# Carrying a run's last quarter of output and the next run's transposed tokens over the loop's back edge

## The chip, the core and the metric

The kernel runs on one NeuronCore of a Trainium2 chip. The metric is the device time of one execution in microseconds (us). Before the change it was 9271.71 us, the median of three runs (9268.06 to 9273.82).

The engines are called by these names: TensorE (PE in the profile, with its weight loads as PEld), VectorE (DVE), ScalarE (ACT), GpSimd (POOL) and SyncE (SP). SP issues the plain transfers. GpSimd issues the indirect ones: gathers of rows by a list of row numbers, and scatters to such rows.

## What is computed

The input is 4 x 1024 tokens of 1024 channels in float32. First an attention-like layer changes every token; then a mixture of experts with 8 experts does, each token going to its best two. The kernel's time lies almost wholly in the second part. Cut to what matters:

```python
x = x + xattn(layernorm(x), ctx_512, W_k, b_k, ln_gamma, ln_beta)   # first part, about 500 us
h = layernorm(x)                                                    # 4096 tokens of 1024
probs = softmax(h @ gate_w)                                         # 8 experts
topk_w, topk_idx = top_k(probs, 2);  topk_w /= topk_w.sum(-1)
# for every expert e, over the tokens that chose it:
y_e = (silu(h @ w1[e]) * (h @ w3[e])) @ w2[e]                       # 1024 -> 3584 -> 1024
x = x + sum of topk_w * y_e over the token's two experts
```

## The kernel before

**First part.** Attention, normalisation and routing run tile by tile. They leave the attended tokens in the output tensor (`of` in the code), the normalised tokens in `h_d`, and in `id_d` one list per expert: the token's row number, and its weight as raw bits beside it.

**Runs and blocks.** The rest of the kernel is a loop on the chip, `tc.For_i`. One pass is a run: one expert and some of its tokens. A `Switch` picks one of 13 unrolled bodies by the number of blocks in the run and their width; each body is what `run(...)` emits. With this input there are 8 runs, one for each expert, of three blocks each, with widths of 328, 336, 352 and 360 tokens. Within a body the compiler's planner orders the work of VectorE, ScalarE, GpSimd and SP by its own estimate of times; TensorE's order is the order of the code (`manual_schedule`).

At the loop's end there is a barrier: every engine arrives, semaphores are set back, and each engine branches to the loop's head, loads the next run's expert, slot and kind from small tables into registers and branches into the body. The barrier and these branches appear in the records at L784, L787 and L815.

**The products.** Every product is done in blocks of two by two with seven products instead of eight (the Winograd form of Strassen's scheme). That takes sums of the four quarters of a weight tile, by `weight_sums` (lines 573 to 577, four VectorE instructions), and sums of the four quarters of the tokens, by `token_sums` (lines 592 to 594, three instructions). The seven products go to four PSUM banks, and `combine` (lines 608 to 614) puts the four quarters of the result together with one ScalarE copy and four VectorE instructions. Half a block's width, `n`, is what one matmul streams.

**A block.** A block has two phases:

- Up: for each of 14 pairs of hidden tiles, a 1 MB tile of `w1` and one of `w3` are loaded, summed and multiplied with the tokens `x` (L735, 56 matmul records for each tile); `combine` gives `c1` and `c3`, then SiLU and product give `g`.
- Down: for each of the four output quarters `q`, four tiles of `w2` are multiplied with `g` (L766), and `combine` gives `y`.

**Tokens in.** `tokens_in` transposes the gathered `rows` on TensorE (L679), 24 transposes in six PSUM tiles, of which the pool holds two at a time. Three are copied to `x` by ScalarE (L687) and three by VectorE (L685). Then come the token sums. For the second and third block it stands after quarter 1 of the block before. For a run's first block it stands at the head of the body.

**Tokens out.** `tokens_out` transposes a quarter's `y` back (L697, six transposes in three PSUM tiles of the same pool) and adds it, times the token's weight, to the accumulator `acc` (L701). After the last quarter three scatters write `acc` to the output rows (L707). The list `late` puts this work behind the next piece of products: quarter `q` is transposed after the first weight tile of quarter `q + 1`, and the last quarter of a block after the first `w1` tile of the next block. After a run's last block it is done at once, at the end of the body. `acc` is filled by gathers from the output tensor (L638) before the down phase.

**Across the edge.** `load_first(i + 1)`, called between the phases of a run's last block, loads the next run's ids, gathers its first rows, and loads its first tiles `w1a` and `w3a`. Their sums and the transposes of the rows are made in the next pass, at the head of the body.

Of the kernel before, what the change touches and what calls it, by code (L numbers as in the profile page):

```python
# [18 lines left out]
P = 128  # L19
# [14 lines left out]
def kernel(  # L34
# [488 lines left out]

    with ExitStack() as st:
        fst = st.enter_context(tc.tile_pool(name="fst", bufs=1))
        wp = st.enter_context(tc.tile_pool(name="wp", bufs=3))
        ap = st.enter_context(tc.tile_pool(name="ap", bufs=1))
        hp = st.enter_context(tc.tile_pool(name="hp", bufs=1))  # L530
        gp = st.enter_context(tc.tile_pool(name="gp", bufs=2))
        ip = st.enter_context(tc.tile_pool(name="ip", bufs=2))
# [7 lines left out]
        RT = 3  # L540
        HK = KD // 2
        NI = KM // 2


        T1, B11, B12, B21, B22, T2, T4 = range(7)
# [12 lines left out]
            weights(t, wf, ex, k0, kn, c0)  # L558
            return t

        def weight_sums(t, kn, halves):

            n = kn // 2
            if halves:
                v = t[:, :kn, :].rearrange("p (i h) c -> p i h c", h=2)
                lo, hi = v[:, :, 0, :], v[:, :, 1, :]
            else:
                lo, hi = t[:, :n, :], t[:, n:kn, :]
            a11, a21 = lo[:, :, :P], lo[:, :, P:]
            a12, a22 = hi[:, :, :P], hi[:, :, P:]  # L570
            s = wp.tile([P, 3, HK, P], F32, tag="s", name="ws")
            s1, s2, s4 = s[:, 0, :n, :], s[:, 1, :n, :], s[:, 2, :n, :]
            nc.vector.tensor_tensor(s1, a21, a22, ALU.add)  # L573
            nc.vector.tensor_tensor(s2, s1, a11, ALU.subtract)  # L574
            nc.vector.tensor_tensor(s4, a12, s2, ALU.subtract)  # L575
            s3 = a21
            nc.vector.tensor_tensor(s3, a11, a21, ALU.subtract)  # L577
            return dict(p1=a11, p2=a12, p3=s4, p4=a22, p5=s1, p6=s2, p7=s3)

        RIGHT = dict(p1=B11, p2=B21, p3=B22, p4=T4, p5=T1, p6=T2, p7=T3)  # L580
        BANK = dict(p1=(0, 0), p2=(1, 0), p6=(1, 1), p5=(2, 0), p7=(2, 1), p3=(3, 0), p4=(3, 1))
# [14 lines left out]
        def banks():  # L596
            return [ps.tile([P, N], F32, tag="ps", name=f"ps{i}") for i in range(4)]

        def combine(pp, n, tag):

            def pair(t):
                return t[:, : 2 * n].rearrange("p (a b) -> p a b", b=n)

            def twice(v):
                return v.unsqueeze(1).to_broadcast([P, 2, n])

            p1s = gp.tile([P, n], F32, tag="p1s", name="p1s")
            nc.scalar.copy(p1s, pp[0][:, :n])  # L608
            c = gp.tile([P, 4, n], F32, tag=tag, name=tag)
            nc.vector.tensor_tensor(c[:, 0:2, :], pair(pp[1]), twice(p1s), ALU.add)  # L610
            vu = gp.tile([P, 2, n], F32, tag="vu", name="vu")
            nc.vector.tensor_tensor(vu, pair(pp[2]), twice(c[:, 1, :]), ALU.add)  # L612
            nc.vector.tensor_tensor(c[:, 1:3, :], pair(pp[3]), vu, ALU.add)  # L613
            nc.vector.tensor_tensor(c[:, 3, :], pp[2][:, :n], vu[:, 1, :], ALU.add)
            return c

        def expert(i):
            return nc.values_load(
# [29 lines left out]
        rows = [fst.tile([P, D], F32, name=f"rows{s}") for s in range(RT)]  # L648
        w1a = fst.tile([P, KD, QW], F32, name="w1a")
        w3a = fst.tile([P, KD, QW], F32, name="w3a")  # L650

        def load_rows(s0):
            load_ids(ids0, s0)
# [4 lines left out]
        def load_first(i):  # L658
            ex = expert(i)
            load_rows(first_slot(i))  # L660
            weights(w1a, w1f, ex, 0, KD, 0)
            weights(w3a, w3f, ex, 0, KD, 0)

        def run(i, ex, s0, blocks, width):
            n = width // 2
            split = [min(P, width - c) for c in range(0, width, P)]

            def tokens_in():

                ids = ip.tile([P, RT, IDW], I32, tag="ids", name="ids")  # L670
                nc.vector.tensor_copy(ids, ids0)
                rd = ip.tile([P, RT], I32, tag="rd", name="rd")
                nc.vector.tensor_copy(rd, rd0)
                x = hp.tile([P, HK, 7 * n], F32, tag="x", name="x")
                for s, r in enumerate(split):
                    for h in range(2):
                        pt = pst.tile([P, N], F32, tag="pt", name="pt_h")
                        for k in range(HK):
                            nc.tensor.transpose(  # L679
                                pt[:, ts(k, r)], rows[s][:r, ts(HK * h + k, P)], ident[:r, :r]  # L680
                            )
                        src = pt[:, : HK * r].rearrange("p (a b) -> p a b", b=r)
                        dst = x[:, :, ds((B11 + 2 * h) * n + s * P, r)]
                        if h % 2:
                            nc.vector.tensor_copy(dst, src)  # L685
                        else:
                            nc.scalar.copy(dst, src)  # L687
                xv = x.rearrange("p k (q c) -> p k q c", q=7)
                token_sums(xv, n)
                return ids, rd, xv  # L690

            def tokens_out(ids, acc, q, y):
                yv = y.rearrange("p (d h) c -> p d (h c)", h=2)
                for s, r in enumerate(split):
                    pt = pst.tile([P, N], F32, tag="pt", name="pt_y")
                    for d in range(2):
                        nc.tensor.transpose(  # L697
                            pt[:r, ts(d, P)], yv[:, d, ds(s * P, r)], ident
                        )
                    part = acc[s][:r, ts(q, QW)]  # L700
                    nc.vector.scalar_tensor_tensor(  # L701
                        part, pt[:r, :QW], ids.bitcast(F32)[:r, s, 1:2], part,
                        ALU.mult, ALU.add,
                    )
                if q == DQ - 1:
                    for s, r in enumerate(split):
                        nc.gpsimd.indirect_dma_start(  # L707
                            out=of,
                            out_offset=bass.IndirectOffsetOnAxis(
                                ap=ids[:r, s, 0:1], axis=0  # L710
                            ),
                            in_=acc[s][:r, :],
                            in_offset=None,
                            bounds_check=T - 1,
                            oob_is_err=False,
                        )

            late = []
            now = tokens_in()
            for b in range(blocks):  # L720
                ids, rd, x = now
                last = b == blocks - 1
                if not last:
                    load_rows(s0 + (b + 1) * width)
# [1 line left out]
                for i2 in range(NI):  # L726
                    cs = []
                    for wf, wa, tag in ((w1f, w1a, "c1"), (w3f, w3a, "c3")):
                        t = load(wf, ex, 0, KD, i2 * QW) if b or i2 else wa
                        left = weight_sums(t, KD, False)  # L730
                        pp = banks()
                        for p in ORDER if b or i2 else EARLY:
                            bk, half = BANK[p]
                            for k in range(HK):
                                nc.tensor.matmul(  # L735
                                    pp[bk][:, ts(half, n)], left[p][:, k, :],
                                    x[:, k, RIGHT[p], :],
                                    start=(k == 0), stop=(k == HK - 1),
                                )
                        cs.append(combine(pp, n, tag))  # L740
                        while late:
                            late.pop(0)()
                    c1, c3 = cs
                    nc.scalar.activation(c1, c1, AF.Silu)  # L744
                    nc.vector.tensor_tensor(g[:, i2, B11 : B22 + 1, :], c1, c3, ALU.mult)  # L745
                    token_sums(g[:, i2, :, :], n)

                if last:
                    load_first(i + 1)
                acc = [  # L750
                    ap.tile([P, D], F32, tag=f"acc{s}", name="acc") for s in range(len(split))
                ]
                for s, r in enumerate(split):
                    gather(acc[s][:r, :], of, rd, s, r)
                for q in range(DQ):
                    pp = banks()
                    i2 = 0
                    for kn in W2K:
# [13 lines left out]
                            i2 += 1  # L772
                        while late:
                            late.pop(0)()
                    y = combine(pp, n, "y")
                    late.append(lambda a=ids, c=acc, d=q, e=y: tokens_out(a, c, d, e))
                    if q == 1 and not last:
                        now = tokens_in()
            while late:
                late.pop(0)()  # L780

        load_first(0)
        n_run = nc.values_load(run_n, min_val=1, max_val=NRUN)
        with tc.For_i(0, n_run) as i:  # L784
            ex = expert(i)
            s0 = first_slot(i)
            kind = nc.values_load(run_k[:, ds(i, 1)], min_val=0, max_val=len(RUNS) - 1)  # L787
            for k in tc.Switch(kind, len(RUNS)):
                with tc.manual_schedule(engines={ENG.PE}):
                    run(i, ex, s0, *RUNS[k])  # L790


# [26 lines left out]
```

## Time and profile before

| what | value |
|---|---|
| median of three timed runs | 9271.71 us |
| profiled execution, its own time | 9277.28 us |
| span of that execution in the profile | 9275.4 us |
| mean granted TensorE clock | 0.977 |
| TensorE matmul busy | 8865.5 us, 96% of the span |
| VectorE busy | 5115.8 us, 55% |
| ScalarE, GpSimd busy | 694.4 us, 406.0 us |
| bytes moved by transfers | 1236.36 MB, mean 133 GB/s |

The profile is one execution. A window such as 8142.56:8177.57 is a stretch in us from the span's start. A row of windows gives the stretch's length, and then for each engine its busy time with the number of instructions in brackets, the clock that TensorE was granted (1.00 is full speed), the share of time in which the transfer engines were busy, and GB/s. A row of waits names who waited, for whom, the total in us, how often, and the longest. One fp32 matmul of the code is two records of about 0.15 us each in the trace, from start to start.

The last of the seven edges between runs, in order of time (from the sequencers' and engines' records):

| us | what |
|---|---|
| 8142.56 | last matmul of the down phase starts |
| 8143.24 | VectorE starts the last instruction of `combine` |
| 8144.94, 8151.67, 8155.84 | the three scatters start, each after the one before has landed |
| 8150.05, 8150.25 | VectorE and TensorE arrive at the barrier |
| 8164.00 | GpSimd has drained, as the last |
| 8171.01 | first transpose of the next run's tokens |
| 8177.57 | first matmul of the up phase |

### The profile page before, as it was taken

The page shows a single profiled execution, that of the slowest core. Times are in us where ns is not written, and L with a number is a line of the kernel's source. Part 1 is how long each engine was busy: PE and PEld are TensorE (multiplying, and loading weights), DVE is VectorE, ACT ScalarE, POOL GpSimd, SP SyncE. Part 2 cuts the span into 40 slices and gives each one's busy share as a digit, 9 for nine tenths or more (in the row PEclk, how much of TensorE's full clock was granted, in tenths as well). Part 3 has the DMA queues.
Part 4 walks back from the last instruction along what each step waited for, and adds up shares of the span by engine and source line. Part 5 has one row for each costly group of instructions (what it writes and reads, how often), then busy time and mean ns, then how long its engine had stood idle before and what let it go on. Part 6 is the DMA issues. An engine that isn't in the chain of part 4 may idle for free. (4 is left out here: it accounts for less than half of the span.)

```text
span 9275.4 us, 139976 instructions
## 1 busy us (share of the span) xinstructions
PE 8865.5 (96%) x59428; PEld 8665.9 (93%) x59429; DVE 5115.8 (55%) x10003; ACT 694.4 (7%) x1524; POOL 406.0 (4%) x494
## 2 busy tenths in 40 slices
PE   8979998999989999899989999899998999989999
PEld 5569998999989999899989999899998999989999
DVE  5655654655645555556546556465564565555654
ACT  3300000000000000000000000000000000000000
POOL 2310000000000000000000000000000000000000
PEclk9979999999999999999999999999999999999999
DMA  3234444344433444344434434444443344434343
GB/s 132 109 123 145 138 144 141 125 147 130 157 118 118 143 131 138 119 136 138 141 128 135 139 121 138 132 132 146 137 147 120 125 140 135 141 117 141 124 134 127
DMA packets 1116668, 1236.36 MB, mean 133 GB/s; under 512 B 34848, under 2 KB 1077280, under 8 KB 1115872
## 3 DMA queue, kind: packets, MB, share of 16 engines
q1 hardware_dynamic: 1079424, 1114.54, 37.1%
q0 software_dynamic: 31952, 107.24, 3.3%
q8 instruction: 500, 8.19, 0.4%
q10 hardware_dynamic: 4496, 3.97, 0.1%
q14 instruction: 296, 2.42, 0.1%
HBM read 1155.26 MB, written 70.65 MB: 132 GB/s over the span
## 5 line engine op out<-in xcount | busy, mean ns | idle before, releaser
L735 PE MATMUL ps<-x,wt 128*128 128x168 f32 (+3 forms) x20992 | 3285.3, 309 | 0.0
L735 PEld LDWEIGHTS ps<-x,wt 128*128 128x128 f32 x20992 | 3123.4, 190 | 0.0
L735 PE MATMUL ps<-x,ws 128*128 128x168 f32 (+3 forms) x16128 | 2571.8, 309 | 0.0
L735 PEld LDWEIGHTS ps<-x,ws 128*128 128x128 f32 x16128 | 2411.8, 190 | 0.0
L766 PE MATMUL ps<-g,wt 128*128 128x168 f32 (+3 forms) x10752 | 2031.6, 310 | 0.0
L573 DVE TENSOR_TENSOR ws<-wt 128x512 f32<-128x512 f32 (+1 forms) x1040 | 693.8, 667 | 2206.3 <-DMA wt<-in_L_ffn_w_dram 2123.3
L766 PEld LDWEIGHTS ps<-g,wt 128*128 128x128 f32 x10752 | 1693.4, 191 | 0.0
L766 PE MATMUL ps<-g,ws 128*128 128x168 f32 (+3 forms) x8064 | 1619.6, 310 | 0.0
L766 PEld LDWEIGHTS ps<-g,ws 128*128 128x128 f32 x8064 | 1299.0, 191 | 0.2 <-DVE y L610 0.2
L610 DVE TENSOR_TENSOR c<-ps,p1s 128x352 f32<-128x352 f32 (+3 forms) x672 | 346.7, 516 | 1045.1 <-PE ps L735 1016.1
L574 DVE TENSOR_TENSOR ws<-ws,wt 128x512 f32<-128x512 f32 (+1 forms) x1040 | 692.4, 666 | 30.2
L577 DVE TENSOR_TENSOR wt<-wt 128x512 f32<-128x512 f32 (+1 forms) x1040 | 685.3, 659 | 0.0
L575 DVE TENSOR_TENSOR ws<-wt,ws 128x512 f32<-128x512 f32 (+1 forms) x1040 | 684.3, 658 | 0.0
L608 ACT COPY p1s<-ps 128x168 f32<-128x168 f32 (+3 forms) x768 | 228.5, 298 | 5319.3 <-PE ps L766 2881.0
L744 ACT ACTIVATE c<-c 128x672 f32<-128x672 f32 (+3 forms) x336 | 261.6, 778 | 2559.5 <-DVE c L613 2543.4
L613 DVE TENSOR_TENSOR c<-ps,vu 128x352 f32<-128x352 f32 (+3 forms) x672 | 344.6, 513 | 43.2 <-PE ps L735 36.2
L679 PE MATMUL pt_h<-ident,rows 128*128 128x128 f32 (+4 forms) x576 | 98.3, 319 | 272.7 <-DVE ws L573 128.4
L612 DVE TENSOR_TENSOR vu<-ps,c 128x352 f32<-128x352 f32 (+3 forms) x672 | 342.2, 509 | 17.5 <-PE ps L735 17.5
L679 PEld LDWEIGHTS pt_h<-ident,rows 128*128 128x128 f32 (+4 forms) x576 | 74.9, 169 | 295.0 <-issue 240.3
L745 DVE TENSOR_TENSOR g<-c,c 128x672 f32<-128x672 f32 (+3 forms) x336 | 294.1, 875 | 11.3
L638 POOL DMA_INDIRECT rows<-h_d,rd x75 | 78.1, 1042 | 4180.1 <-DVE ws L574 4136.0
L707 POOL DMA_INDIRECT out_dram<-acc,ids x72 | 74.0, 1028 | 4136.6 <-DVE acc L701 3929.3
(165 smaller groups left out, 3073.3 us busy)
## 6 DMA issues: line engine op xcount, KB each, us to landing
wt<-in_L_ffn_w_dram SPq DMA_DIRECT2D x848, 1024.0 KB, 5.1
wt<-in_L_ffn_w_dram SPq DMA_DIRECT2D x192, 768.0 KB, 4.7
xt<-in_x_dram SPq DMA_DIRECT2D x32, 512.0 KB, 4.4
out_dram<-x SPq DMA_DIRECT2D x32, 512.0 KB, 2.9
h_d<-hn SPq DMA_DIRECT2D x32, 512.0 KB, 2.6
w1a<-in_L_ffn_w_dram SPq DMA_DIRECT2D x9, 1024.0 KB
w3a<-in_L_ffn_w_dram SPq DMA_DIRECT2D x9, 1024.0 KB, 11.9
cx<-in_ctx_dram SPq DMA_DIRECT2D x4, 1024.0 KB, 9.9
```

Of the source, the lines that this page charges most:

```text
L573: nc.vector.tensor_tensor(s1, a21, a22, ALU.add)
L574: nc.vector.tensor_tensor(s2, s1, a11, ALU.subtract)
L575: nc.vector.tensor_tensor(s4, a12, s2, ALU.subtract)
L577: nc.vector.tensor_tensor(s3, a11, a21, ALU.subtract)
L608: nc.scalar.copy(p1s, pp[0][:, :n])
L610: nc.vector.tensor_tensor(c[:, 0:2, :], pair(pp[1]), twice(p1s), ALU.add)
L612: nc.vector.tensor_tensor(vu, pair(pp[2]), twice(c[:, 1, :]), ALU.add)
L613: nc.vector.tensor_tensor(c[:, 1:3, :], pair(pp[3]), vu, ALU.add)
L735: nc.tensor.matmul(pp[bk][:, ts(half, n)], left[p][:, k, :], x[:, k, RIGHT[p], :], start=(k == 0), stop=(k == HK - 1),)
L744: nc.scalar.activation(c1, c1, AF.Silu)
L745: nc.vector.tensor_tensor(g[:, i2, B11 : B22 + 1, :], c1, c3, ALU.mult)
L766: nc.tensor.matmul(pp[bk][:, ts(half, n)], left[p][:, k, :], g[:, i2, RIGHT[p], :], start=(i2 == 0 and half == 0), stop=(i2 == NI - 1 and ...
```

## The change

A run's last quarter of output is no longer transposed, added and scattered at the end of the body. `combine` writes it to a fixed tile `y1`, with the token numbers and weights kept in `ids1`, and `leftover()` does the rest: it is the first entry of `late` in the next pass, so it comes after that run's first `w1` tile, and it stands once more after the loop. In the first pass it works on zeros, with row numbers that are out of bounds and are left out by the scatter. Columns beyond the run's width get such numbers too. `acc`, `y1` and `ids1` are set before the loop by GpSimd.

The transposes of the next run's first tokens, and the sums of its `w1a`, move from the head of the body to the last block, behind quarter 1, where the other blocks have theirs; for the first run they stand before the loop. As the next run's width isn't known there, `tokens_in` always transposes 3 x 128 rows into a fixed tile `x` of 384 columns. The token sums depend on the width and stay at the head of the body, now as `token_factors`: four VectorE instructions into a tile `xs` of their own, one of them over `x` in place. The sums of `w1a` have a tile of their own, `s1a`. The sums of `w3a` stay where they were. `y` has one buffer instead of two, and `combine` writes its four quarters with the distance that the fixed tile has.

The core of the diff (the tiles' allocation, and the same lines of `combine` and `weight_sums` with other names, are left out):

```diff
-        def weight_sums(t, kn, halves):
+        def factors(t, kn, halves, s):
...
+        def weight_sums(t, kn, halves, s=None):
+            if s is None:
+                s = wp.tile([P, 3, HK, P], F32, tag="s", name="ws")
+            f = factors(t, kn, halves, s)
+            a11, a12, a21, a22 = f["p1"], f["p2"], f["p7"], f["p4"]
+            nc.vector.tensor_tensor(f["p5"], a21, a22, ALU.add)
+            nc.vector.tensor_tensor(f["p6"], f["p5"], a11, ALU.subtract)
+            nc.vector.tensor_tensor(f["p3"], a12, f["p6"], ALU.subtract)
+            nc.vector.tensor_tensor(a21, a11, a21, ALU.subtract)
+            return f
...
+        ids1 = fst.tile([P, RT, IDW], I32, name="ids1")
+        nc.gpsimd.memset(ids1, NONE)
+        acc = [fst.tile([P, D], F32, name=f"acc{s}") for s in range(RT)]
+        for a in acc:
+            nc.gpsimd.memset(a, 0.0)
+        y1 = fst.tile([P, 2 * XW], F32, name="y1")
+        nc.gpsimd.memset(y1, 0.0)
...
+        def tokens_in():
+            for s in range(RT):
+                for h in range(2):
+                    pt = pst.tile([P, N], F32, tag="pt", name="pt_h")
+                    for k in range(HK):
+                        nc.tensor.transpose(
+                            pt[:, ts(k, P)], rows[s][:, ts(HK * h + k, P)], ident
+                        )
...
+        def token_factors(n):
+            b11, b12 = x[:, :HK, :n], x[:, :HK, n : 2 * n]
+            b21, b22 = x[:, HK:, :n], x[:, HK:, n : 2 * n]
+            t1, t2, t4 = (xs[:, :, j, :n] for j in range(3))
+            nc.vector.tensor_tensor(t1, b12, b11, ALU.subtract)
+            t3 = b12
+            nc.vector.tensor_tensor(t3, b22, b12, ALU.subtract)
+            nc.vector.tensor_tensor(t2, b22, t1, ALU.subtract)
+            nc.vector.tensor_tensor(t4, b21, t2, ALU.subtract)
+            return dict(p1=b11, p2=b21, p3=b22, p4=t4, p5=t1, p6=t2, p7=t3)
...
+        def leftover():
+            tokens_out(ids1, [P] * RT, DQ - 1, y1)
+
         def run(i, ex, s0, blocks, width):
...
-            late = []
-            now = tokens_in()
+            late = [leftover]
+            right = token_factors(n)
             for b in range(blocks):
-                ids, rd, x = now
+                ids, rd = take_ids()
...
-                        left = weight_sums(t, KD, False)
+                        if t is w1a:
+                            left = factors(w1a, KD, False, s1a)
+                        else:
+                            left = weight_sums(t, KD, False)
...
                 if last:
                     load_first(i + 1)
-                acc = [
-                    ap.tile([P, D], F32, tag=f"acc{s}", name="acc") for s in range(len(split))
-                ]
+                    beyond = ip.tile([P, RT], F32, tag="beyond", name="beyond")
+                    nc.vector.tensor_scalar(
+                        beyond, at, float(width), float(NONE), ALU.is_ge, ALU.mult
+                    )
+                    nc.vector.tensor_tensor(ids1[:, :, 0], beyond, ids[:, :, 0], ALU.add)
+                    nc.vector.tensor_copy(ids1[:, :, 1], ids[:, :, 1])
...
-                    y = combine(pp, n, "y")
-                    late.append(lambda a=ids, c=acc, d=q, e=y: tokens_out(a, c, d, e))
-                    if q == 1 and not last:
-                        now = tokens_in()
-            while late:
-                late.pop(0)()
+                    if last and q == DQ - 1:
+                        combine(pp, n, y1, XW)
+                        break
+                    y = gp.tile([P, 2 * XW], F32, tag="y", name="y", bufs=1)
+                    combine(pp, n, y, XW)
+                    late.append(lambda a=ids, d=q, e=y: tokens_out(a, split, d, e))
+                    if q == 1:
+                        tokens_in()
+                        if last:
+                            weight_sums(w1a, KD, False, s1a)
+                        else:
+                            right = token_factors(n)
 
         load_first(0)
+        tokens_in()
+        weight_sums(w1a, KD, False, s1a)
         n_run = nc.values_load(run_n, min_val=1, max_val=NRUN)
         with tc.For_i(0, n_run) as i:
...
+        leftover()
```

## The prediction

> **What bounds the kernel now.** I read the page first, then the list of waits on TensorE, then windows around every place where TensorE pauses. The page says that TensorE is the bound:
>
> ```profile
> PE 8865.5 (96%) x59428; PEld 8665.9 (93%) x59429; DVE 5115.8 (55%) x10003; ACT 694.4 (7%) x1524; POOL 406.0 (4%) x494
> ```
>
> VectorE has 45% of the span free, so work added there costs only where TensorE waits for it. The longest wait of TensorE stands before the token transposes of a run, up to 25.9 us each time:
>
> ```profile
> PE pt_h L679 <- DVE ws L573: 128.4, 5, 25.9
> ```
>
> There are eight runs, so seven edges between runs. I measured each from the start of the last down-projection matmul (L766) to the start of the first up-projection matmul (L735) and asked for those windows (columns: length, then each engine's busy time, granted clock, DMA):
>
> ```profile
> 1567.79:1608.08 40.29, 6.49 (x33) 4.89 (x32) 8.36 (x18) 2.88 (x4) 7.13 (x7) 0.57 0.24 78
> ...
> 8142.56:8177.57 35.01, 6.72 (x33) 5.07 (x32) 8.43 (x18) 2.94 (x4) 7.28 (x7) 0.57 0.29 90
> sum 250.22, PE 46.48 PEld 35.04 DVE 59.08 ACT 20.43 POOL 50.92; mean PE 6.64 PEld 5.01 DVE 8.44 ACT 2.92 POOL 7.27
> ```
>
> So the seven edges hold 250.2 us. The last one, cut at its events, shows what fills it: 2.3 us of output transposes, 26.1 us without TensorE (first three scatters, then barrier and branches), 6.6 us of token transposes:
>
> ```profile
> 8142.56:8144.90 2.34, 1.16 (x9) 0.63 (x7) 1.88 (x5) 0.00 (x0) 0.00 (x0) 1.00 0.01 4
> 8144.90:8160.10 15.20, 0.24 (x2) 0.00 (x0) 0.63 (x2) 0.00 (x0) 2.94 (x3) 0.59 0.29 99
> 8160.10:8171.00 10.90, 0.00 (x0) 0.00 (x0) 1.39 (x5) 0.00 (x0) 0.27 (x1) 0.50 0.04 10
> 8171.00:8177.57 6.57, 5.32 (x24) 4.44 (x25) 4.52 (x9) 2.94 (x4) 4.07 (x4) 0.50 0.79 231
> ```
>
> Two more views price the moved work: phases of the last two runs, and the clock in the first 6 us after an edge (third column from the end):
>
> ```profile
> 8411.71:8537.23 125.52, 122.85 (x828) 121.22 (x827) 51.97 (x98) 2.88 (x7) 2.94 (x3) 1.00 0.41 131
> ...
> 8021.95:8142.56 120.61, 119.53 (x804) 118.79 (x803) 45.11 (x88) 1.23 (x4) 0.00 (x0) 1.00 0.34 106
> 8177.57:8411.71 234.14, 234.14 (x1569) 234.14 (x1568) 149.91 (x281) 19.59 (x43) 2.93 (x2) 1.00 0.41 133
> 8537.23:8772.56 235.33, 234.76 (x1577) 234.51 (x1575) 149.98 (x286) 18.29 (x42) 6.77 (x6) 1.00 0.42 138
> ```
>
> ```profile
> 5993.26:5999.26 6.00, 6.00 (x31) 6.00 (x30) 4.28 (x6) 0.30 (x1) 2.78 (x2) 0.67 1.05 394
> 7063.58:7069.58 6.00, 6.00 (x36) 6.00 (x35) 5.76 (x8) 0.31 (x1) 2.93 (x2) 0.83 1.05 388
> 8177.57:8183.57 6.00, 6.00 (x40) 6.00 (x39) 5.75 (x8) 0.31 (x1) 2.93 (x2) 0.94 1.04 390
> ```
>
> **The change, part by part.** The sum is made against the profiled execution: 9277.3 us, a span of 9275.4 and 1.9 around it. It lies 5.6 us above the median of the three timed runs, 9271.7, and I carry the difference over.
>
> *The edge (7 times).* The scatters and both groups of transposes leave it. What stays I take from the sequencer records of the edge at 8142.56. TensorE's branch back took 4.96 us (8145.23 to its arrival at 8150.25). Without output transposes TensorE is free to branch at about 8142.7, and arrives near 8148.1. VectorE's last combine now starts at 8143.24; before, its last operation started at 8145.18 and VectorE arrived at 8150.05, 4.87 us later, so it would arrive at 8148.1 too. SP checks the semaphores earlier than that. GpSimd, which before came last (third scatter at 8155.84, drain from 8161.64 to 8164.00), has had nothing to do since the gathers near 8007, and has drained long before. From the last arrival (8164.0) to TensorE's first operation (8171.01) took 7.0 us: two barriers, register loads, the branch into the case (3.71 us on TensorE), semaphore checks. So the new edge is 5.55 + 0.1 + 7.0 = 12.65 us from matmul to matmul. Saved: 250.2 - 7 x 12.65 = **161.7 us**. Bounds: 10.5 us an edge if TensorE's branch is issued ahead of its queued matmuls, 24.4 if another arrival keeps the barrier late (a rival below).
>
> *The clock (7 times, +10 us).* After 12.65 us of idleness the clock is at half again: at this edge it fell near 8147.6, 5 us after the last matmul. Today the transposes run in much of that half-speed time; the first 6 us of L735 had clocks 0.75, 0.93, 0.78, 0.87, 0.67, 0.83 and 0.94, a loss of 6 x (1 - clock), 7.4 us over seven. The edge's half speed lasted until 7.3 us after its sparse transposes began at 8171.0; now dense matmuls meet it. Worst row: clock 0.67, 2.0 us lost. I take 2.5 us an edge, between that row and a whole 6.6 us at half speed (3.3), so 7 x 2.5 - 7.4 = 10; bounds 0 and 16.
>
> On the clock a rule stands against this change. The Trainium skill ("TensorE: Matmul & The Clock Gate", Part 1) says that the clock halves after an idle window of about 3.4 us and comes back only after a busy one. The trace agrees in kind (clock 0.50 from 8160 to 8177); an estimate by that page would be 1.7 us for one cold window, 7 x 1.7 - 7.4 = +4.5, and the sum would be 5.5 us better than mine.
>
> *Tokens into the last block (8 times, +42.5 us).* Twenty-four transposes, six copies (three on ScalarE, three on VectorE) and, hidden, four weight sums of 0.68 us on VectorE follow quarter 1 of each run's last block; the eighth is for a run that never comes. The other blocks have it there already: a down phase took 125.52 us with it and 120.61 without at the same width, 4.9 us. Over all sixteen such phases, each against its run's last block, the mean is 5.3 (4.4 to 6.6). 8 x 5.3 = 42.5; bounds 35 and 53. Its inputs are there: ids, w1a and w3a transfers were issued at 7998 and the rows' gathers from 8004 to 8008, some 75 us ahead of quarter 1's end.
>
> *Leftover in the first block (8 times, +17.6 us).* Six transposes and three multiply-adds now follow the first matmul group; the first pass works on zeros. A phase with such late work took 235.33 us against 234.14 without: 1.2 us. At a run's start I add 1 us: three 1 MB weight transfers and the gathers fill the DMA engines there (1.04 to 1.05 share above), VectorE's queue holds weight sums that wait for them, and the third transpose pair waits for the first multiply-add. The longest such pause of TensorE at later blocks was 2.4 us. So 8 x 2.2 = 17.6; bounds 1.2 and 5 each, 9 to 40. The scatters then run beside matmuls: some 14.5 us on GpSimd's queue, with the accumulators' gathers behind them, which are needed only some 235 us later.
>
> *VectorE, hidden.* Token sums become four instructions at about 0.87 us for three (1.59, 0.87, 0.87), a second table of ids adds three small ones, and one output buffer instead of two leaves 20 us between its last reader and next writer. The first up phase has VectorE busy for 149.9 of 234.1 us. Uncovered, the edge's part would cost 3.5 us a run: the first sum is needed after 12 products, 3.6 us of TensorE, and takes 0.9.
>
> *Start and end (+9 us).* In the first pass the branch into the case ran while TensorE waited for the rows (landed 553.4). Now the transposes end near 560 and the register loads, branch (3.43 us) and checks follow: 6 us; bounds 0 and 10. The memsets fit GpSimd's pause from 532 to 544. At the end the loop is left before the last output is transposed: 3 us of semaphore checks; bounds 2 and 7.
>
> Sum: -161.7 + 10 + 42.5 + 17.6 + 6 + 3 = **-82.6 us**. 9271.7 - 82.6 = **9189 us** (9194.7 for a profiled execution like this one).
>
> **The rivals.** *The edge shrinks less.* The first edge is 5 us longer than the others, with a GpSimd drain of up to 7.8 us, so an arrival can be late for reasons not seen here. At 17.65 us an edge the gain is 35 less: 9224. Against it: GpSimd is idle for 130 us before the edge.
>
> *The edge does not shrink* (the change doesn't do what it says). If branches, not scatters, hold the barrier, the 26.1 us stay and only transposes leave: 26.9 us an edge, 62 saved, 79 paid, 9289. It turns against the change at 24.4 us an edge. Against it: TensorE, VectorE and ScalarE arrived by 8150.3 and waited 14 us for GpSimd's scatters.
>
> *Slower: the leftover waits for weights.* If VectorE's queue has the sums of the third weight tile ahead of the multiply-add, TensorE stands until they are done. That tile's sums started at 8194.19, 23.4 us after the loads' first issue at 8170.80; TensorE would want the result some 11.3 us after the start. That is a stop of 13.3 us, 12.3 beyond mine, 8 x 12.3 = 98: 9287. It decides from 10.3 us a run. For it: full DMA engines. Against: without the early accumulator gathers 4.5 MB come first, not 6, and later blocks put the multiply-add promptly.
>
> **How the numbers follow.** My case has 0.72 (its own range 9160 to 9222), the shorter saving 0.14, the stop behind weights 0.07, the unshortened edge 0.04, something between that ends within 0.2% 0.03. A change of 0.2%, 18.5 us, is about what a measurement of this kernel can tell from none. Faster 0.72 + 0.14 = 0.86, same 0.03, slower 0.11. The range leaves out the two slow cases and the last corners of the bounds: from 9155 (edges of 10.5 us, +15, and cheaper terms, +19) to 9238 (9224 plus a leftover dearer by 1.7 us eight times).
>
> **What would show it.** Right: seven edges near 12.6 us with no scatter and no pt_h in them; scatters of the leftover 12 to 30 us into each run; down phases of last blocks near 125.5 us at 352 tokens; the first up phase about 3 us longer than now; GpSimd arriving at the barrier first. Wrong: edges over 17 us, or a stop of TensorE at pt_y of more than 5 us in the first block, released by VectorE's weight sums.

## The result, and the profile after

The changed kernel takes 9152.7 us (median; 9149.3 to 9158.1), against 9272.8 us before in the same series: a ratio of 0.9871, 95% interval 0.9854 to 0.9888. That is 120 us less, where 83 were forecast, and 2.3 us below the forecast's range. A later series gave the changed kernel 9152.6 us, ratio 0.9874 (0.9857 to 0.9890).

The first part of the page after, engines by busy time and share of the span:

```profile
span 9147.6 us, 139985 instructions
...
PE 8852.5 (97%) x59458; PEld 8654.2 (95%) x59459; DVE 5120.9 (56%) x10062; ACT 697.9 (8%) x1527; POOL 409.4 (4%) x503
```

The seven edges, again from the start of a run's last down-projection matmul (now L815) to the first up-projection matmul of the next (L776); the columns are length, busy time of PE, PEld, DVE, ACT and POOL, granted clock, DMA share, GB/s:

```profile
1575.71:1586.69 10.98, 0.30 (x3) 0.05 (x2) 2.03 (x6) 0.00 (x0) 0.00 (x0) 0.63 0.05 12
...
8034.82:8045.76 10.94, 0.32 (x3) 0.06 (x2) 2.17 (x7) 0.00 (x0) 0.00 (x0) 0.74 0.05 11
sum 75.61, PE 2.15 PEld 0.37 DVE 12.50 ACT 0.00 POOL 0.00; mean PE 0.31 PEld 0.05 DVE 1.79 ACT 0.00 POOL 0.00
```

GpSimd and ScalarE have no work at an edge any more, and the seven edges hold 75.6 us, not 250.2. The first is no longer longer than the rest. At the last edge the leftover's three scatters start 12.4 to 22.7 us into the run, beside the matmuls. What was paid for it stands in the phases. The last block's down phase and the next first up phase, at 352 tokens:

```profile
7909.42:8034.82 125.40, 122.73 (x827) 121.19 (x826) 47.05 (x91) 2.98 (x7) 0.00 (x0) 1.00 0.32 102
8045.76:8283.12 237.36, 236.89 (x1573) 236.65 (x1574) 152.20 (x290) 20.84 (x44) 9.31 (x9) 0.99 0.43 143
```

They were 120.61 and 234.14 us before. Cutting both profiled executions at the same matmuls gives the whole account. Each is one execution; the one before lay 4.5 us above its median, the one after 3.5 below, so their difference is 127.8 us and not 120.

| stretch | before | after | difference | forecast |
|---|---|---|---|---|
| to the first L735 / L776 | 560.4 | 561.6 | +1.3 | +6 |
| seven edges | 250.2 | 75.6 | -174.6 | -161.7 |
| eight first up phases | 1838.2 | 1864.3 | +26.1 | +27.6 (clock 10, leftover 17.6) |
| sixteen other up phases | 3691.6 | 3684.4 | -7.3 | 0 |
| eight last down phases | 942.7 | 980.6 | +37.9 | +42.5 |
| sixteen other down phases | 1972.4 | 1964.1 | -8.3 | 0 |
| from the last matmul of a down phase to the end | 19.8 | 16.9 | -2.9 | +3 |
| sum | 9275.4 | 9147.6 | -127.8 | -82.6 |

### The profile page after: what moved, and what is told of

The parts are those of the page before. It is cut to its first block, busy times and chain, and to the rows that moved or that the text cites. A ratio compares the mean times of both kernels' runs of the same rounds, so it can differ in the third digit from the quotient of the medians.

```text
span 9147.6 us, 139985 instructions
## 1 busy us (share of the span) xinstructions
PE 8852.5 (97%) x59458; PEld 8654.2 (95%) x59459; DVE 5120.9 (56%) x10062; ACT 697.9 (8%) x1527; POOL 409.4 (4%) x503
## 5 line engine op out<-in xcount | busy, mean ns | idle before, releaser
L776 PE MATMUL ps<-x,wt 128*128 128x168 f32 (+3 forms) x15744 | 2510.5, 309 | 0.0
L776 PEld LDWEIGHTS ps<-x,wt 128*128 128x128 f32 x15744 | 2353.5, 190 | 0.0
L815 PE MATMUL ps<-g,wt 128*128 128x168 f32 (+3 forms) x10752 | 2027.1, 309 | 0.0
L815 PEld LDWEIGHTS ps<-g,wt 128*128 128x128 f32 x10752 | 1688.8, 190 | 0.0
L776 PE MATMUL ps<-xs,ws 128*128 128x168 f32 (+3 forms) x10624 | 1659.2, 309 | 0.0
L815 PE MATMUL ps<-g,ws 128*128 128x168 f32 (+3 forms) x8064 | 1615.4, 309 | 0.0
L776 PEld LDWEIGHTS ps<-xs,ws 128*128 128x128 f32 x10624 | 1579.1, 190 | 0.0
L815 PEld LDWEIGHTS ps<-g,ws 128*128 128x128 f32 x8064 | 1294.7, 190 | 0.3 <-DVE y L620 0.2
L776 PE MATMUL ps<-x,ws 128*128 128x168 f32 (+3 forms) x5312 | 883.2, 309 | 0.0
L776 PE MATMUL ps<-xs,wt 128*128 128x168 f32 (+3 forms) x5248 | 872.6, 309 | 0.0
L776 PEld LDWEIGHTS ps<-x,ws 128*128 128x128 f32 x5312 | 804.1, 190 | 0.0
L776 PEld LDWEIGHTS ps<-xs,wt 128*128 128x128 f32 x5248 | 794.4, 190 | 0.0
```

The costliest lines, as they stand in the source:

```text
L776: nc.tensor.matmul(pp[bk][:, ts(half, n)], left[p][:, k, :], right[p][:, k, :], start=(k == 0), stop=(k == HK - 1),)
L815: nc.tensor.matmul(pp[bk][:, ts(half, n)], left[p][:, k, :], g[:, i2, RIGHT[p], :], start=(i2 == 0 and half == 0), stop=(i2 == NI - 1 and ...
```

## The experiments

My theory, as forecast: the scatters held the barrier, so the output carry brings the gain, and the token carry trades some 7 us at an edge for some 5 us in a block. The rivals: branches hold the barrier; or each half brings its share. What the account left open were the edges, shorter than I had worked out, and the blocks in between, which the change hardly touches and which got 15.6 us shorter.

**The output carry alone.** The tokens of a run's first block go back to the head of the body:

```diff
             late = [leftover]
+            tokens_in()
+            weight_sums(w1a, KD, False, s1a)
             right = token_factors(n)
...
-                    if q == 1:
+                    if q == 1 and not last:
                         tokens_in()
-                        if last:
-                            weight_sums(w1a, KD, False, s1a)
-                        else:
-                            right = token_factors(n)
+                        right = token_factors(n)
...
         load_first(0)
-        tokens_in()
-        weight_sums(w1a, KD, False, s1a)
```

> The output carry alone: the next run's tokens are transposed at the head of the body again, at 128 rows each, and the sums of w1a are made there too. Theory (the scatters held the barrier; a transposed block of tokens costs about as much at the head as behind quarter 1): the seven edges rise from 10.8 us to about 17.4 us (the 6.6 us of transposes come back), the eight last blocks' down phases fall back by 38 us in all, the first up phases lose less to the half-speed clock (about 8 us), the start is 4 us shorter: 46 - 38 - 8 - 4, so 9149 us, level with the changed kernel to within 10 us. Rival (branches and barrier hold the edge, not the scatters): the edges stay near 33 us and the time near 9270 us. Rival (each half of the change is worth its share of the gain): about 9190 us.

Measured: 9145.1 us, ratio 0.9866 (0.9849 to 0.9882). Its edges:

```profile
1561.53:1579.76 18.23, 5.90 (x27) 4.81 (x26) 7.30 (x18) 3.04 (x4) 2.31 (x2) 0.60 0.30 92
...
8028.72:8046.82 18.10, 5.91 (x28) 4.81 (x26) 7.32 (x18) 3.04 (x4) 2.31 (x2) 0.63 0.29 93
sum 128.27, PE 41.22 PEld 33.53 DVE 51.23 ACT 21.29 POOL 16.14; mean PE 5.89 PEld 4.79 DVE 7.32 ACT 3.04 POOL 2.31
```

The edges are 18.3 us each, 0.9 more than expected, and the transposes' 5.9 us of TensorE are seen in them. The last down phases are back at 943.1 us in sum and the time is level with the changed kernel. The first up phases fall by 19.0 us, where 8 were expected: measured against the usual step from record to record, the first 56 matmul records of the eight runs lose 4.6 us in place of 18.7, and the leftover costs less too (1.55 us from matmul to matmul in the mean, 2.17 in the changed kernel). Both rivals fall: this half has the whole gain.

**The token carry alone.** The last quarter is transposed, added and scattered at the end of the body:

```diff
-            late = [leftover]
+            late = []
...
                     if last and q == DQ - 1:
                         combine(pp, n, y1, XW)
+                        tokens_out(ids, split, q, y1)
                         break
...
                     run(i, ex, s0, *RUNS[k])
-        leftover()
```

> The token carry alone: a run's last quarter is transposed, added and scattered at the end of the body as before. Theory: the edges fall from 35.7 us only by the 6.6 us of transposes and some 0.7 us of checks, to about 28.5 us, which saves 50 us; the eight last blocks pay 38 us, the colder first up phases 10 us, the start 4 us: level with the kernel before, 9275 us, or some 15 us less (9260 us) if the short spells of half-speed clock inside the blocks are gone because all transposes are 128 rows wide. Rival (the half of the gain is here): 9210 us or less.

Measured: 9270.8 us, ratio 0.9999 (0.9989 to 1.0009). The windows of its edges:

```profile
1572.14:1605.32 33.18, 1.37 (x10) 0.61 (x8) 3.60 (x10) 0.00 (x0) 2.97 (x3) 0.56 0.14 46
...
8139.36:8166.19 26.83, 1.40 (x10) 0.64 (x8) 3.12 (x7) 0.00 (x0) 2.94 (x3) 0.57 0.18 59
sum 195.97, PE 9.69 PEld 4.39 DVE 20.66 ACT 0.00 POOL 20.69; mean PE 1.38 PEld 0.63 DVE 2.95 ACT 0.00 POOL 2.96
```

With the three scatters in them the edges are 28.0 us each, and the first is again 6 us longer than the rest. Half of the change removes 54 us of edges and makes the kernel no faster: 37.9 us come back in the last blocks' down phases and 22.4 us in the first up phases, where 10 were expected. These begin at half clock (17.5 us lost in the first 56 matmul records of the runs, 8.8 before), and there are pauses of up to 2.6 us behind VectorE that the kernel before doesn't have:

```profile
PEld ps L776 <- DVE c L624: 10.4, 7, 2.6
```

On the 15 us that I had left open: the sixteen other down phases are 8.1 us shorter than before and the profile has no spell of half clock in them, so that gain is here too; the dearer first up phases have eaten it.

**The last combine left out.** Why are the edges 10.8 us and not 12.65? In the records of the edge at 8034.82 TensorE arrives at the barrier at 8037.73, ScalarE at 8038.60 and VectorE, last, at 8039.46; GpSimd goes on at 8039.57. TensorE's branch back was issued at 8032.83, 2.0 us before its last matmul started, so it arrives 2.9 us after that start, not the 5.5 that I had taken. VectorE comes to its branches at 8035.25 and 8035.90, around the start of its last combine instruction (8035.50), and arrives 3.56 us after the second. At the edge at 8142.56 of the kernel before that way took 4.20 us (8145.85 to 8150.05). To see whether VectorE sets the edge, its last work was taken away:

```diff
                     if last and q == DQ - 1:
-                        combine(pp, n, y1, XW)
                         break
```

> The changed kernel without the combine of each run's last output quarter; that quarter is left out of the result (y1 stays zero), everything else is computed. Theory (the edge now starts when VectorE arrives at the barrier, 4.6 us after the last matmul, because its branch back is issued only behind the last combine; TensorE arrives after 2.9 us): without that combine TensorE is last, and the seven edges fall from 10.8 us to about 9.1 us, 12 us in all. Rival (TensorE's or SP's own way round sets the edge): they stay at 10.8 us.

Measured in a single run: 9142.2 us. The edges:

```profile
1574.68:1583.58 8.90, 0.31 (x4) 0.07 (x2) 0.33 (x1) 0.00 (x0) 0.00 (x0) 0.68 0.03 8
...
8027.56:8036.43 8.87, 0.31 (x4) 0.06 (x2) 0.00 (x0) 0.00 (x0) 0.00 (x0) 0.78 0.03 7
sum 62.24, PE 2.18 PEld 0.42 DVE 1.94 ACT 0.00 POOL 0.00; mean PE 0.31 PEld 0.06 DVE 0.28 ACT 0.00 POOL 0.00
```

8.9 us an edge. VectorE's combine was what the edge waited for; without it TensorE's arrival, 2.7 to 3.1 us after its last matmul's start, is left, and then register loads, a branch of 3.3 to 4.2 us into the body and one check.

**Narrow transposes put back.** The profile before has eight spells of 3.4 us at half clock inside the blocks, six of them behind token transposes; the profile after has none. The change makes all third groups of transposes 128 rows wide; before they were 72 to 104. This kernel goes back to narrow ones in the first and second block of a run:

```diff
-        def tokens_in():
+        def tokens_in(split=(P, P, P)):
...
-                            pt[:, ts(k, P)], rows[s][:, ts(HK * h + k, P)], ident
+                            pt[:, ts(k, r)], rows[s][:r, ts(HK * h + k, P)], ident[:r, :r]
...
-                        tokens_in()
+                        tokens_in([P] * RT if last else split)
```

> The changed kernel with one thing put back: in the first and second block of a run the third group of transposes is again only as wide as the block needs (72 to 104 rows), as in the kernel before. Theory (the narrow transposes let a window of the clock gate count as idle): of the sixteen places some 3 to 7 show a spell of 3.4 us at half clock again, each 1.6 us longer than its neighbours; the time rises by 5 to 11 us at most. Rival (those spells came from where the free-running window happened to fall, or from elsewhere): none of them returns, or they come in the last blocks too, which are still wide.

> The kernel before once more, for a second profile of it: do the eight short spells of half clock inside the blocks return, and at the same blocks? If they are set by the program, about eight return, mostly behind quarter 1 of blocks of 336 and 352 tokens; if by chance, their number and places differ freely. The edges should again be about 35 us each, 250 us in all, and the time within 9 us of 9272 us.

Measured: the narrow version 9159.2 us (two runs), ratio 0.9880 (0.9860 to 0.9900), which overlaps the changed kernel's, so the time alone says nothing; the kernel before again 9275.4 us, its edges 249.0 us in sum. Eight microseconds from the start of token transposes, first the narrow version at a spell, then the changed kernel at the same width (clock in the third column from the end):

```profile
5103.37:5111.37 8.00, 6.51 (x38) 5.73 (x37) 7.99 (x15) 1.65 (x3) 0.00 (x0) 0.79 0.34 99
```

```profile
5463.11:5471.11 8.00, 6.41 (x47) 5.68 (x46) 7.82 (x15) 1.76 (x3) 0.00 (x0) 1.00 0.31 98
```

The narrow version has two such spells behind token transposes, in sixteen places; I had expected three to seven. The second profile of the kernel before has seven in sixteen (six in the first), mostly at other blocks than in the first profile, so the program doesn't fix the places. Counted over all profiles of this study whose transposes stand behind a quarter in one piece, narrow ones have 15 spells in 48 places and wide ones 1 in 144. The Trainium skill ("TensorE: Matmul & The Clock Gate", Part 1) says that the gate watches activity in free-running windows of 3.4 us; the runs agree, with spells that are 3.41 us or a multiple of it long and that move from execution to execution. The counts go with the width. But 13 of the 15 come from the kernel before (13 in 32 places); the version that changes nothing but the width has 2 in 16, so other differences between the two kernels may have a part. That the narrow transposes count as less activity is a possible reason, not a shown one.

**The leftover later.** It goes behind the third pair of tiles:

```diff
-            late = [leftover]
+            late = []
...
                         while late:
                             late.pop(0)()
+                    if b == 0 and i2 == 2:
+                        late.append(leftover)
                     c1, c3 = cs
```

> The changed kernel with the leftover work put behind the third pair of w1 and w3 tiles of a run in place of the first w1 tile. Theory (at a run's head VectorE's queue holds weight sums that wait for three transfers at once, so that TensorE's third pair of output transposes waits 0.7 to 2.2 us for VectorE, mean 1.4): later in the phase the pauses fall to about 0.6 us, the first up phases are 0.8 us shorter each, 6 us in all. Rival (the pauses belong to the leftover wherever it is): no change beyond 2 us. The rest of the first up phase's 3.3 us, the colder clock, stays.

Measured: 9143.5 us, ratio 0.9859 (0.9843 to 0.9874). From matmul to matmul across the leftover it is now 1.57 to 1.75 us; in the changed kernel it was 1.48 to 2.94, mean 2.17, and 2.63 in its second profile. The eight first up phases sum to 1860.0 us, 4.3 less than the changed kernel's profile and 10.5 less than its second. The crowd at a run's head did cost, about 0.6 to 1 us a run, where 0.8 was expected; the time alone (9 us, intervals that overlap) could not have shown it.

**In pieces.** The account prices a token block at 4.7 us and the pauses between its transposes are in the trace: each waits until a copy has emptied one of two PSUM tiles. Over the whole of the changed kernel the list of waits of the weight loads has, for the output and the token transposes:

```profile
PEld pt_y L726 <- DVE acc L728: 71.2, 97, 2.2
...
PEld pt_h L699 <- ACT x L707: 44.7, 62, 0.9
```

Two versions spread this work. In the first, `tokens_in` returns six pieces of four transposes, and at most two are done behind one `w2` tile:

```diff
...
                     if q == 1:
-                        tokens_in()
+                        late += tokens_in()
                         if last:
-                            weight_sums(w1a, KD, False, s1a)
+                            late.append(lambda: weight_sums(w1a, KD, False, s1a))
                         else:
-                            right = token_factors(n)
+                            late.append(lambda: right.update(token_factors(n)))
...
```

> A version meant to be faster: tokens_in in six pieces of four transposes, at most two pieces behind one w2 tile from quarter 2 on, so that TensorE never waits for a PSUM tile of the pool of two. Theory (of the 5 us that a tokens_in costs, 24 transposes take 2.6 us at full clock and the rest are pauses for the copies): 2.3 us less in each of 24 blocks, 55 us, about 9098 us. Rival (the transposes themselves, or refilling TensorE's queue after each piece, are the cost): less than 15 us.

In the second, `tokens_out` returns three pieces too, each with its own scatter after the last quarter, and every tile, up and down, is followed by at most two pieces:

```diff
+            def some():
+                for _ in range(2):
+                    if late:
+                        late.pop(0)()
...
-                        while late:
-                            late.pop(0)()
+                        some()
...
-                    late.append(lambda a=ids, d=q, e=y: tokens_out(a, split, d, e))
+                    late += tokens_out(ids, split, q, y)
```

> As the kernel with tokens_in in pieces, and tokens_out in three pieces too, two behind one weight tile and the third behind the next. Theory (of the 1.2 us of each tokens_out, 0.66 us are transposes and 0.5 us a pause in which the third pair waits for VectorE to empty a PSUM tile): 0.5 us less in each of 96, another 48 us, about 9050 us. Rival (the pause only moves to the next tile): no more than 10 us beyond tokens_in in pieces.

Measured: 9102.1 us, ratio 0.9817 (0.9803 to 0.9830), and 9030.2 us, ratio 0.9739 (0.9726 to 0.9752), the best kernel of the study. The first saves 50.6 us against the changed kernel, where 55 were expected. The waits of the weight loads for the accumulators in the first, then the same waits and those for the token transposes in the second:

```profile
PEld pt_y L731 <- DVE acc L733: 71.1, 97, 2.5
```

```profile
PEld pt_y L732 <- DVE acc L734: 1.0, 1, 1.0
...
PEld pt_h L698 <- DVE x L704: 0.6, 2, 0.4
...
PEld pt_h L698 <- ACT x L706: 0.4, 2, 0.3
```

71.1 us of waits for the accumulators have become 1.0, and that is the step from the first version to the second: 71.9 us in the time, 69.8 between the two profiled spans. I had expected 48, having priced every pause at the usual 0.5 us; those behind a crowded VectorE are up to 2.5 us and go too.

**Is the token carry worth having?** The output carry alone was level with the whole change. The last kernel takes the token carry out of the version in pieces:

```diff
             late = leftover()
+            at_once(tokens_in())
+            weight_sums(w1a, KD, False, s1a)
             right = token_factors(n)
...
-                    if q == 1:
+                    if q == 1 and not last:
                         late += tokens_in()
-                        if last:
-                            late.append(lambda: weight_sums(w1a, KD, False, s1a))
-                        else:
-                            late.append(lambda: right.update(token_factors(n)))
+                        late.append(lambda: right.update(token_factors(n)))
...
         load_first(0)
-        at_once(tokens_in())
-        weight_sums(w1a, KD, False, s1a)
```

> The version with everything in pieces, but with the first block's tokens transposed at the head of the body again (no token carry). Theory (the token carry only trades one price for another: 7.5 us less at each of seven edges against what a tokens_in costs in eight last blocks plus 5 us for the colder clock and 4 us at the start; in pieces it costs 2.6 us in place of 4.8): without it 7 x 7.5 - 8 x 2.6 - 9 = 23 us slower than everything in pieces, 9053 us, where the same step made the changed kernel 7 us faster. Rival (the carry of the tokens is worth nothing in either form): 9030 us within 6 us.

> The changed kernel once more, beside the version without the token carry, for a closer time and a second profile: 9152 us, seven edges near 10.8 us, and, if wide transposes keep the clock up, at most one short spell of half clock behind the 24 groups of token transposes.

Measured: 9041.7 us, ratio 0.9757 (0.9741 to 0.9773), beside the changed kernel's 9152.6 us in the same series. It is 0.0018 above the best one's ratio, 17 us; the intervals overlap, but the two accounts bear it out: the profiled spans differ by 12.5 us. Without the carry the edges are 130.7 us against 75.6 (+55), the last down phases 929.3 against 950.4 (-21), the first up phases 1837.2 against 1853.0 (-16) and the start 552.1 against 559.9 (-8). The sign is as expected, the size smaller: the first up phases without the cold clock are worth 16 us, not 5 (2.5 us lost in the first 56 matmul records of the runs, 18.3 with the carry). Of the 8 us at the start 4 belong to the carry, as expected (from the first token transpose to the first matmul 7.0 us, with it 11.0); the rest is where the first part ended. The second profile of the changed kernel has edges of 75.9 us in sum and no spell behind its 24 groups of token transposes.

## Why the prediction was right or wrong

**The mechanism was right.** The scatters held the barrier, and the output carry alone, measured by itself, has the whole gain (9145.1 us; the token carry alone 9270.8). GpSimd began its drain at 7904.46, 130 us ahead of the edge at 8034.82. The rivals "the edge does not shrink" and "the leftover waits for weights" are refuted: the edges are 10.8 us, and no wait of the output transposes for VectorE exceeds 2.2 us in this profile (3.1 in the second).

**The step that failed by most is "TensorE arrives near 8148.1 and VectorE too", with the 7.0 us behind the last arrival: the edge of 12.65 us.** TensorE's branch was timed from a record in which it stood behind output transposes that waited for VectorE. With these gone it was issued 2.0 us ahead of the last matmul, and TensorE arrives after 2.9 us, not 5.5. But VectorE is the last to arrive, and for it the step failed in another way. It was priced at 4.87 us from the start of its last instruction; that took 4.0 us. Its last branch took 3.5 to 3.7 us at the seven edges, 4.0 to 5.2 before. Over all runs it took 3.9 to 5.3 us in the three profiles with output transposes and scatters at the edge, and 3.45 to 3.89 in the eight without; why is not shown. So the last arrival comes 4.7 us after the last matmul's start in the mean, 0.9 less than worked out. The other 1.0 us lies behind it, 6.1 us in place of 7.1: the checks at the head of the body shrink from ten to one (1.03 us before, from 8169.98 to 8171.01; 0.09 at the edge at 8034.82). Together that is 1.85 us an edge and 12.9 us of the profiles' 45.2 us of error.

That the bound of 10.5 lay so near 10.8 is luck. It was drawn from an early branch of TensorE alone, and by my own figure for VectorE, 8148.1, that would have changed nothing.

**The second is "a token block costs 5.3 us, and nothing changes in the other blocks".** The mean of 5.3 had the spells of half clock in it, 1.6 us each. I listed the wide transposes as part of the change and gave them no price. In the changed kernel the spells are gone: a token block costs 4.7 us in the last blocks (4.6 us of the error), and the sixteen other down phases lose 8.3 us.

**Start and end** were 4.7 and 5.9 us too dear. From the first token transpose to the first matmul the start is 10.9 us where it was 6.7, so 4.2 and not 6; the rest is where the first part happened to end. At the end the check of all semaphores now lies ahead of the last scatter and not behind it; the two halves show it, 16.9 us with the output carry alone and 19.8 with the token carry alone.

**The clock and the leftover were right, the clock partly by luck.** In the first 56 matmul records of each run, measured against the usual step, 18.7 us are lost where 8.8 were: +9.9, against a forecast of 10. The Trainium skill's window alone ("TensorE: Matmul & The Clock Gate", Part 1) gave an estimate of 1.7 us an edge; the runs show 2.3, because the half clock went on for 3.0 to 6.2 us after a restart, 4.6 in the mean. The first 6 us behind the last edge, where the row before had a clock of 0.94:

```profile
8045.76:8051.76 6.00, 6.00 (x25) 6.00 (x26) 5.25 (x12) 2.87 (x3) 1.21 (x1) 0.63 0.50 153
```

That +9.9 came so close to 10 is chance: the second profiles have 16.2 and 12.2, so +4.0. The leftover is 16.2 us (8 x 2.02, one usual step taken off each), against 17.6; in the second profile it is 19.8.

**Open:** 7.3 us in the sixteen other up phases. Their sum lies between 3683 and 3692 us in the ten profiles without output in pieces, with the longest pauses at output transposes in different places each time. Of the 7.3 us, 4.8 lie in two phases that in the profile before have a spell of half clock and in the profile after have none (228.0 us each, now 225.9 and 225.3). No run tells apart whether the change has a part in it. And 8 us of the error are no error of the sum: the two profiled executions stood on opposite sides of their medians.

**The range** missed by 2.3 us because its lower end joined the shortest edge to some cheaper terms, but held the other phases at exactly nothing; they gave 15.6 us.

## What to carry to other kernels

At a barrier only the last arrival counts: find which engine's wait ends last, and move that work behind the next pass's first products; work that merely stands beside it there may move for nothing, as the token carry did until its transposes were spread. TensorE's branch that followed no wait was issued 2.0 us ahead of its last matmul, so don't price a branch from a record in which it stood behind a wait. And before moving transposes, look at what they wait for: two PSUM tiles and bursts of six and of 24 transposes cost 120 us here, which spreading them, at most two pieces behind a weight tile, took away.

## What the runs showed of the hardware that was not expected

The granted clock fell to half for 3.4 us inside dense phases in 15 of 48 places where a burst of transposes ended with groups of 72 to 104 rows, and in 1 of 144 where all groups had 128 rows. Each cost about 1.6 us.

VectorE's branch to the loop's end took 3.93 to 5.29 us at 21 edges that had output transposes and scatters, and 3.45 to 3.89 us at 56 edges that had none.
